# One graph-attention kernel, second attention of a group: two tasks of two banks joined into one task of four banks

## Chip, cores, metric

The kernel runs on one core of one Trainium2 chip. The metric is device time in microseconds (us). TensorE is PE below, ScalarE ACT, VectorE DVE, GpSimd POOL. In this kernel matmuls read tiles in the memory called SBUF and write their results into "banks", tiles in the memory called PSUM; reading a finished bank out with ACT or DVE is called its evacuation. Times are medians of unprofiled and profiled executions of one call; a profile is one execution. All runs told of here were in the fast state, with a granted TensorE clock of 0.998 or 0.999 of full speed.

## The reference

Inputs are 128 graphs of 64 nodes with 512 features, one shared adjacency matrix, and the weights of one layer. Cut to what matters:

```python
def gat_heads(x, adj, W, a):                     # W: [H, F, O]
    Wh = einsum('bnf,hfo->bhno', x, W)
    f1 = einsum('bhno,ho->bhn', Wh, a[:, :O]); f2 = ... a[:, O:]
    e = f1[..., :, None] + f2[..., None, :]
    e = where(e > 0, e, 0.01 * e)                # leaky ReLU
    e = where(adj[None, None] > 0, e, -1e9)
    return einsum('bhnm,bhmo->bhno', softmax(e), Wh)

h   = relu(layernorm(x))
h1  = elu(gat_heads(h, adj, W_heads, a_heads))   # four heads, then concatenated
out = elu(gat_heads(h1, adj, W_out, a_out))      # the second attention
y   = relu(out @ w1 + b1) @ w2 + b2 + out
return x + layernorm(y)
```

## The kernel before

The 128 graphs are worked through in 16 groups of 8. Each large product is done as seven smaller block products, p = 1, 5, 6, 2, 3, 7, 4 in that order. One product p of one head is a "step" on PE: four f32 matmuls of 256 columns, which leave eight records in the trace. Blocks c11, c12, c21, c22 of the result come out of sums of the banks g1, g5, g6 (DVE) and of copies s1, s5, t (ACT). Shortened:

```python
def after(p):                                    # evacuation of product p
    if p in (1, 5, 6):
        if p == 6:
            nc.vector.tensor_tensor(gb[6], gb[6], sb["s1"], ALU.add)
        nc.scalar.copy(sb[nm], gb[p])            # s1, s5 or t
    elif p == 2: post("c11", gb[1])
    elif p == 7: post("c22", gb[6], sb["s5"], gb[1])     # c22 = g6 + s5
    elif p == 3: post("c12", gb[5], sb["t"], gb[5])
    else:        post("c21", gb[6])              # p = 4 adds into bank g6

def elu(dst, src, name):                         # three scratch tiles
    ex = wk.tile([P, 512], FP, tag="elu", name=f"ex{name}", bufs=3)
    nc.scalar.activation(ex, src, AF.Relu, scale=-1.0)
    nc.scalar.activation(ex, ex, AF.Exp, scale=-1.0)
    nc.vector.scalar_tensor_tensor(dst, ex, -1.0, src, ALU.add, ALU.max)
```

So p = 4 of a head may not start before the DVE addition c22 has read g6. Each head's last product, p = 4, is put off ("late") into the next head's second step; that of the last head falls into the next product, `project2`, whose pieces of g_b are on PE by then:

```python
return [
    s[0], lambda: (s[1](), flush_late()), lambda: (s[2](), next_sums()), s[3], s[4],
    lambda: (s[5](), late.append(s[6])),
]                                                # next_sums: three GpSimd subtractions
...
    flush_late()                                 # after the last head
```

The second attention of the group before runs beside these steps, from a list of entries spread evenly over the 24 steps of the four heads (`gap` is an empty entry):

```python
def attend2(g, q):                               # half a group: two banks
    pa = [aux([P, FO], ...) for b in range(NB)]
    ... 4 matmuls of 64 x 64 tiles, 512 columns each ...
    for b in range(NB):
        elu(OUT[g][:, 2 * q + b], pa[b], f"2_{g}_{q}_{b}")

gap + score + [lambda: spread2(g)] + gap * 2 + [lambda: softmax2(g)] + gap * 5
+ [lambda: transpose_weights2(g)] + gap * 2 + attend[0:1] + gap * 2 + attend[1:2] + gap * 4
```

The second softmax has two operations that will matter. L435 is the leaky ReLU, which reads the tile `e` twice; L453 multiplies a mask by the reciprocal sums. Both have both inputs in SBUF:

```python
nc.vector.scalar_tensor_tensor(ei, ei, ALPHA, ei, ALU.mult, ALU.max)          # L435
...
nc.vector.tensor_tensor(rb, blkones[...], r[...], ALU.mult)                   # L453
```

Of the kernel before, what the change touches and what calls it, by code (L numbers as in the profile page):

```python
# [9 lines left out]
FP = mybir.dt.float32  # L10
# [12 lines left out]
def gat_preln_kernel(  # L23
# [31 lines left out]
    P = 128  # L55
# [3 lines left out]
    FO = W_out.shape[1]  # L59
    DF = w1.shape[1]  # L60
    NB = P // N
    KC = F // P
    NT = B * N // P
    G = 4
# [9 lines left out]
    big = ctx.enter_context(tc.tile_pool(name="big", bufs=1))  # L74
# [5 lines left out]
    def bank(name):  # L80
        return ps.tile([P, 2, T], FP, tag="mm", name=name)

    def flat(ap):
        return ap.rearrange("p a b -> p (a b)")
# [8 lines left out]
    def aux(shape, name):  # L93
        return ps.tile(shape, FP, tag="aux", name=name, bufs=2)
# [473 lines left out]
    def elu(dst, src, name):  # L568
# [5 lines that stand above are left out]
# [130 lines left out]
    A2, AT2, F2, OUT = {}, {}, {}, {}  # L704

    def scores2(g, j):
        if j == 0:
            F2[g] = sm.tile([P, 2, G], FP, tag="f2", name=f"f2_{g}")
        f = F2[g]
        for c in range(2):  # L710
            junk = wk.tile([P, FO], FP, tag="elu", name=f"jf{g}_{j}_{c}", bufs=3)
            nc.vector.scalar_tensor_tensor(
                junk, WH2[g][:, j], 1.0, ao[:, c, :], ALU.mult, ALU.mult,
                accum_out=f[:, c, j:j + 1],
            )

    def spread2(g):

        f = F2[g]
        dg = sm.tile([P, G, N], FP, tag="s2dg", name=f"s2dg{g}", bufs=1)  # L720
        nc.vector.tensor_tensor(
            dg, eye[:, None, :].to_broadcast([P, G, N]), f[:, 1][:, :, None].to_broadcast([P, G, N]),
            ALU.mult,
        )
        F2[g] = f, dg

    def softmax2(g):
        f, dg = F2.pop(g)
        pe = aux([P, G, N], f"s2pe{g}")
        nc.tensor.matmul(  # L730
            pe.rearrange("p h m -> p (h m)"), blkones.rearrange("p b n -> p (b n)"),
            dg.rearrange("p h m -> p (h m)"), start=True, stop=True,
        )
        A2[g] = softmax(pe, f[:, 0], G, "s2", g)

    def transpose_weights2(g):
        A = A2.pop(g)
        pt = aux([P, G, P], f"s2pt{g}")
        for j in range(G):
            nc.tensor.transpose(pt[:, j, :], A[:, j].rearrange("p b m -> p (b m)"), ident)  # L740
        AT2[g] = wk.tile([P, G, P], FP, tag="hT", name=f"at2_{g}", bufs=4)
        nc.scalar.copy(AT2[g], pt)

    def attend2(g, q):


        if q == 0:
            tag = "out" if g < NG - 1 else "z11"
            OUT[g] = big.tile([P, G, FO], FP, tag=tag, name=f"o{g}")
        pa = [aux([P, FO], f"pa2_{g}_{q}_{b}") for b in range(NB)]  # L750
        for b in range(NB):
            rows = slice(b * N, (b + 1) * N)
            for c in range(2):
                nc.tensor.matmul(
                    pa[b][c * N:(c + 1) * N], AT2[g][rows, 2 * q + c, rows],
                    WH2[g][rows, 2 * q + c, :], start=True, stop=True, skip_group_check=True,
                )
        for b in range(NB):
            elu(OUT[g][:, 2 * q + b], pa[b], f"2_{g}_{q}_{b}")

    def stage_e(g):

        gap = [lambda: None]
        score = [lambda j=j: scores2(g, j) for j in range(G)]
        attend = [lambda q=q: attend2(g, q) for q in range(2)]
        return (
            gap + score + [lambda: spread2(g)] + gap * 2 + [lambda: softmax2(g)] + gap * 5
            + [lambda: transpose_weights2(g)] + gap * 2 + attend[0:1] + gap * 2 + attend[1:2] + gap * 4
        )


# [169 lines left out]
    for g in range(NG):  # L941
        if g >= 1:
            side = stage_e(g - 1)
            done, n = 0, 6 * H
            for i in range(n):
                if i % 6 == 0:
                    steps = project1(g, i // 6)
                steps[i % 6]()
                while done * n < (i + 1) * len(side):
                    side[done]()  # L950
                    done += 1
            flush_late()
# [3 lines left out]
        if g == NG - 1:  # L956
            run(project2(g), tr + [nothing] * 6 + ff[:2])
            run(ff[2:], [
                lambda: [scores2(g, j) for j in range(G)], lambda: spread2(g), nothing, nothing,
                lambda: softmax2(g), *[nothing] * 7, lambda: transpose_weights2(g), nothing,  # L960
                *[lambda q=q: attend2(g, q) for q in range(2)], nothing,
            ])
            continue
# [67 lines left out]
```

## Time and profile before

| | before |
|---|---|
| time, median of 3 runs | 2299.97 us (2298.76 to 2300.67) |
| span of the profiled execution | 2297.4 us |
| busy share PE, DVE, ACT, POOL | 99%, 56%, 39%, 44% |
| distance from one group to the next ("period") | 140.37 us |
| second softmax: L435 on s2e, L453 on s2rb (medians of 16) | 0.42 us, 0.17 us |

PE is busy throughout, so the kernel's time is the sum of the distances between the starts on PE. The period is the sharpest ruler: the distance between the single softmax product (L730) of one group and that of the next. It repeats to 0.03 us over twelve groups. Whole executions are less steady: the first such product starts 178.3 to 181.9 us after the beginning in the eleven profiles (1.7 us of that spread is only that the softmax stands one step later in four of them; a mark ahead of it, the first of the products `pzS`, starts at 126.1 to 128.0 us), and the thirteenth distance is 0.2 to 1.2 us longer than the others (why, was not looked into). I give both, period and time; differences of periods are taken before rounding.

The line of the page for the products that p = 4 belongs to has no idle time in it. Columns: line, engine, operation, tiles, shapes, count, then busy us, mean ns, then idle us before them and its cause.

```profile
L289 PE MATMUL g_a<-z,w 128*128 128x256 f32 x1440 | 341.8, 380 | 0.0
```

The list leaves out waits below about 0.15 us. The 0.1 us that the prediction found before p = 4 is therefore not in it.

### The profile page before, as it was taken

Reading aid. Unit: us, or ns where it says so; the run is one execution under the profiler, and the core shown is the slowest. Engines: PE = TensorE matmul, PEld = TensorE weight load, DVE = VectorE, ACT = ScalarE, POOL = GpSimd, SP = SyncE. Lnnn points to the kernel's source line nnn. Section 1 sums busy time; section 2 is a strip of 40 time slices with the busy share of each in tenths; the row PEclk is TensorE's granted clock in tenths of the full one; section 3 lists DMA queues with packets and bytes.
Section 4 is the critical chain, followed back from the end, with each engine's and each line's share of the span. In section 5 each row is a group of like instructions: output and inputs, shape, how many; then the busy total and the mean of one; then the engine's idle time right before and its main releaser. Section 6 shows DMA issues by size and latency. Waiting matters only on the chain. (4 is left out here: it accounts for less than half of the span.)

```text
span 2297.4 us, 33255 instructions
## 1 busy us (share of the span) xinstructions
PE 2274.2 (99%) x11856; PEld 1892.9 (82%) x11856; DVE 1278.8 (56%) x2226; ACT 904.4 (39%) x1633; POOL 1019.9 (44%) x906
## 2 busy tenths in 40 slices
PE   8999999999999999999999999999999999999997
PEld 4688888888888888888888888888888888888885
DVE  7555554755546555564655546555475554744427
ACT  3435344252442525335253352534425244251512
POOL 7653534435244442644425344353443525533324
PEclk9999999999999999999999999999999999999999
DMA  7554454644546455464544645445454454635543
GB/s 280 197 180 130 146 180 133 183 133 142 176 133 183 137 150 167 133 184 133 161 152 141 181 133 178 132 145 180 132 182 133 143 178 131 183 119 170 161 146 106
DMA packets 255011, 361.14 MB, mean 157 GB/s; under 512 B 23768, under 2 KB 143608, under 8 KB 254848
## 3 DMA queue, kind: packets, MB, share of 16 engines
q1 hardware_dynamic: 249744, 341.16, 48.5%
q0 software_dynamic: 4576, 16.81, 2.0%
q8 instruction: 96, 1.57, 0.3%
q10 hardware_dynamic: 528, 1.05, 0.1%
q14 instruction: 67, 0.55, 0.1%
HBM read 331.66 MB, written 27.26 MB: 156 GB/s over the span
## 5 line engine op out<-in xcount | busy, mean ns | idle before, releaser
L304 PE MATMUL g_b<-w,h 128*128 128x256 f32 x2560 | 593.2, 380 | 0.0
L304 PEld LDWEIGHTS g_b<-w,h 128*128 128x128 f32 x2560 | 481.7, 190 | 64.0 <-issue 2.0
L289 PE MATMUL g_a<-z,w 128*128 128x256 f32 x1440 | 341.8, 380 | 0.0
L289 PE MATMUL g_a<-zs_z,w 128*128 128x256 f32 x1440 | 336.0, 382 | 0.0
L289 PEld LDWEIGHTS g_a<-zs_z,w 128*128 128x128 f32 x1440 | 270.3, 190 | 58.9 <-issue 24.3
L289 PEld LDWEIGHTS g_a<-z,w 128*128 128x128 f32 x1440 | 272.6, 190 | 41.0 <-DVE g_a L603 4.9
L304 PE MATMUL g_b<-w,hS 128*128 128x256 f32 x1024 | 238.2, 380 | 0.0
L607 POOL TENSOR_TENSOR hS<-hS,h 128x512 f32<-128x512 f32 x60 | 78.2, 1303 | 359.7 <-DVE hS L573 359.7
L304 PEld LDWEIGHTS g_b<-w,hS 128*128 128x128 f32 x1024 | 192.3, 190 | 24.7 <-issue 0.2
L571 ACT ACTIVATE exc<-g_a 128x512 f32<-128x512 f32 x240 | 142.5, 594 | 164.3 <-DVE g_a L603 96.3
L573 DVE SCALAR_TENSOR_TENSOR h<-exc,g_a 128x512 f32<-128x512 f32 x180 | 123.6, 687 | 140.8 <-ACT exc L572 140.2
L572 ACT ACTIVATE exc<-exc 128x512 f32<-128x512 f32 x240 | 151.4, 631 | 6.6
L688 POOL TENSOR_TENSOR h<-h,h 128x512 f32<-128x512 f32 x64 | 86.8, 1365 | 138.6 <-PE g_b L304 138.6
L688 POOL TENSOR_TENSOR h<-hS,h 128x512 f32<-128x512 f32 x64 | 81.7, 1277 | 146.7 <-PE g_b L304 146.4
L314 POOL TENSOR_TENSOR zs_z<-zS,z 128x512 f32<-128x512 f32 x60 | 85.1, 1418 | 134.1 <-PE g_a L289 130.8
L489 ACT COPY at<-s1pt 128x512 f32<-128x512 f32 x64 | 34.4, 589 | 272.0 <-PE s1pt L485 272.0
L830 POOL TENSOR_TENSOR xr<-xr,bs 128x512 f32<-128x512 f32 x64 | 98.2, 1538 | 81.5 <-DMA xr<-in_x_dram 44.1
L304 PE MATMUL g_d<-w,rt 128*128 128x256 f32 x512 | 121.8, 380 | 2.1 <-DVE o L822 1.0
L289 PE MATMUL g_c<-ot,w 128*128 128x256 f32 x512 | 122.8, 383 | 0.6 <-DVE ot L792 0.6
L289 PE MATMUL g_a<-zS,w 128*128 128x256 f32 x480 | 113.4, 379 | 0.0
L304 PEld LDWEIGHTS g_d<-w,rt 128*128 128x128 f32 x512 | 97.0, 190 | 17.1 <-DVE o L822 2.3
L315 POOL TENSOR_TENSOR zs_z<-z,zs_z 128x512 f32<-128x512 f32 x60 | 81.2, 1353 | 65.1 <-PE g_a L289 44.4
(164 smaller groups left out, 3553.5 us busy)
## 6 DMA issues: line engine op xcount, KB each, us to landing
w<-tc SPq DMA_DIRECT2D x624, 256.0 KB, 2.7
w<-in_L_gnn_W_out_dram SPq DMA_DIRECT2D x192, 256.0 KB, 2.7
w<-in_L_gnn_W_heads_dram SPq DMA_DIRECT2D x180, 256.0 KB, 3.1
w<-in_L_gnn_w_dram SPq DMA_DIRECT2D x96, 256.0 KB, 2.7
x<-in_x_dram SPq DMA_DIRECT2D x64, 256.0 KB, 4.6
xr<-in_x_dram SPq DMA_DIRECT2D x128, 128.0 KB, 2.7
out_dram<-o SPq DMA_DIRECT2D x128, 128.0 KB, 2.4
tc<-pt POOLq DMA_DIRECT2D x20, 512.0 KB, 4.3
```

The costliest lines, as they stand in the source:

```text
L289: LAST["pe"] = nc.tensor.matmul(bk[:, o, :], w[:, k, ts(o, P)], a[:, k, :], start=start and o == 0 and k == 0, stop=k == 1, skip_group_che ...
L304: LAST["pe"] = nc.tensor.matmul(bk[:, j, :], a[:, k, ts(j, P)], w[:, k, :], start=start and k == 0 and j == 0, stop=i == len(ms) - 1 and k ...
L314: eng.tensor_tensor(s2, s1, a11, ALU.subtract)
L315: eng.tensor_tensor(s4, a12, s2, ALU.subtract)
L489: nc.scalar.copy(AT[t].rearrange("p b h n -> p (b h) n"), pt)
L571: nc.scalar.activation(ex, src, AF.Relu, scale=-1.0)
L572: nc.scalar.activation(ex, ex, AF.Exp, scale=-1.0)
L573: nc.vector.scalar_tensor_tensor(dst, ex, -1.0, src, ALU.add, ALU.max)
L607: nc.gpsimd.tensor_tensor(dst, dst, H1["22"][:, h], ALU.add)
L688: nc.gpsimd.tensor_tensor(dst[:, h], x0[:, h], x1[:, h], ALU.subtract)
L830: nc.gpsimd.tensor_tensor(xr, xr, bs, ALU.add)
```

## The change

The intent is to enter and leave PE's mode of four 64 x 64 tiles once per group, not twice. All eight matmuls of a group stand in one block, into four banks: two from the pool for small results and two from the ring of the large products. The task is placed in the third step of the last head. The list has 24 entries where it had 25.

```diff
--- before.py
+++ after.py
@@ -747,7 +747,17 @@
         if q == 0:
             tag = "out" if g < NG - 1 else "z11"
             OUT[g] = big.tile([P, G, FO], FP, tag=tag, name=f"o{g}")
-        pa = [aux([P, FO], f"pa2_{g}_{q}_{b}") for b in range(NB)]
+        second_attention(g, q, [aux([P, FO], f"pa2_{g}_{q}_{b}") for b in range(NB)])()
+
+    def attend2_all(g):
+
+        OUT[g] = big.tile([P, G, FO], FP, tag="out", name=f"o{g}")
+        pa = [[aux([P, FO], f"pa2_{g}_0_{b}") for b in range(NB)]]
+        pa.append([flat(bank(f"pa2_{g}_1_{b}")) for b in range(NB)])
+        for finish in [second_attention(g, q, pa[q]) for q in range(2)]:
+            finish()
+
+    def second_attention(g, q, pa):
         for b in range(NB):
             rows = slice(b * N, (b + 1) * N)
             for c in range(2):
@@ -755,17 +765,19 @@
                     pa[b][c * N:(c + 1) * N], AT2[g][rows, 2 * q + c, rows],
                     WH2[g][rows, 2 * q + c, :], start=True, stop=True, skip_group_check=True,
                 )
-        for b in range(NB):
-            elu(OUT[g][:, 2 * q + b], pa[b], f"2_{g}_{q}_{b}")
+
+        def finish():
+            for b in range(NB):
+                elu(OUT[g][:, 2 * q + b], pa[b], f"2_{g}_{q}_{b}")
+        return finish
 
     def stage_e(g):
 
         gap = [lambda: None]
         score = [lambda j=j: scores2(g, j) for j in range(G)]
-        attend = [lambda q=q: attend2(g, q) for q in range(2)]
         return (
             gap + score + [lambda: spread2(g)] + gap * 2 + [lambda: softmax2(g)] + gap * 5
-            + [lambda: transpose_weights2(g)] + gap * 2 + attend[0:1] + gap * 2 + attend[1:2] + gap * 4
+            + [lambda: transpose_weights2(g)] + gap * 5 + [lambda: attend2_all(g)] + gap * 3
         )
```

## The prediction

> **What bounds the kernel now.** I read the page first, for the busy shares.
>
> ```profile
> PE 2274.2 (99%) x11856; PEld 1892.9 (82%) x11856; DVE 1278.8 (56%) x2226; ACT 904.4 (39%) x1633; POOL 1019.9 (44%) x906
> ```
>
> The columns are busy us, share of the 2297.4 us span, instructions. TensorE (PE) is the bound. The list of waits puts next to no waiting on PE between 150 and 2020 us (0.5 us in all), the distance from one group's second attention to the next group's is constant (478.71 to 619.08 to 759.44 us, 140.4 each), and the granted clock there is 1.00. So the kernel's time is the sum of the distances between PE's starts, and a change counts by what it does to that sum. Busy shares cannot show it, since ends of matmuls are modelled; I therefore read starts in the timeline of PE around one group's last two tasks. Columns: start, length, engine, line, tiles, shapes, records (an f32 matmul leaves two records).
>
> ```profile
> 485.01 1.89 PE L289 MATMUL g_a<-z,w 128*128 128x256 f32 x8
> 486.83 1.09 PE L754 MATMUL pa<-wh,at 64*64 64x512 f32 x8
> 487.85 1.99 PE L289 MATMUL g_a<-zs_z,w 128*128 128x256 f32 x8
> 489.68 1.89 PE L289 MATMUL g_a<-z,w 128*128 128x256 f32 x8
> 491.41 3.62 PE L289 MATMUL g_a<-zs_z,w 128*128 128x256 f32 x16
> 494.86 1.03 PE L304 MATMUL g_b<-w,h 128*128 128x256 f32 x4
> 495.82 1.99 PE L289 MATMUL g_a<-z,w 128*128 128x256 f32 x8
> ```
>
> A full step of 8 records takes 1.727 us (491.41 to 494.86 is two). The step before the attention takes 1.82, the attention 1.02, the step after it 1.83: the task costs 4.67 - 2 x 1.727 = 1.22 us. Its four 64x64 matmuls run side by side as two passes of 512 columns; two passes at full rate (4 x 0.216, from the 256-column records) would be 0.86. So 0.36 us of a task is getting into and out of the four-tile mode. The second fact is small: the four g_b records at 494.86 should take 0.86, but the next step starts 0.96 later. That is a stall of 0.10 us per group, too short to be listed as a wait.
>
> The first score product is a control for "is that 0.36 paid per block or per pass": eight matmuls of 256 columns, thus four passes, in the same mode.
>
> ```profile
> 540.89 1.89 PE L304 MATMUL g_b<-w,h 128*128 128x256 f32 x8
> 542.71 1.09 PE L405 MATMUL s1pe<-R,L 64*64 64x256 f32 x16
> 543.74 1.99 PE L289 MATMUL g_c<-ot,w 128*128 128x256 f32 x8
> 545.57 2.75 PE L304 MATMUL g_b<-w,h 128*128 128x256 f32 x12
> ```
>
> It costs 545.57 - 540.89 - 2 x 1.727 = 1.23 us against 4 x 0.216 = 0.86: again 0.36, though it has twice the passes. The overhead is paid once per block.
>
> What holds the step at 495.82 is seen on ScalarE (ACT) and VectorE (DVE), three stretches of their timelines in the same group:
>
> ```profile
> 480.20 0.59 ACT L571 ACTIVATE ex<-pa 128x512 f32<-128x512 f32 x1
> 480.68 0.63 ACT L572 ACTIVATE exc<-exc 128x512 f32<-128x512 f32 x1
> 481.20 0.63 ACT L572 ACTIVATE ex<-ex 128x512 f32<-128x512 f32 x1
> ...
> 491.86 0.58 ACT L255 COPY t_a<-g_a 128x512 f32<-128x512 f32 x1 [1.36 <-DVE g_a L254]
> 492.34 0.60 ACT L571 ACTIVATE exc<-g_a 128x512 f32<-128x512 f32 x1
> 492.97 0.63 ACT L572 ACTIVATE exc<-exc 128x512 f32<-128x512 f32 x1
> ```
>
> ```profile
> 491.13 0.69 DVE L254 TENSOR_TENSOR g_a<-g_a,s_a 128x512 f32<-128x512 f32 x1
> 493.63 0.69 DVE L573 SCALAR_TENSOR_TENSOR h<-exc,g_a 128x512 f32<-128x512 f32 x1 [1.81 <-ACT exc L572]
> 494.24 0.69 DVE L603 TENSOR_TENSOR g_a<-g_a,t_a 128x512 f32<-128x512 f32 x1
> 495.06 0.70 DVE L603 TENSOR_TENSOR g_a<-g_a,s_a 128x512 f32<-128x512 f32 x1
> ```
>
> The last product of the last head (p = 4) accumulates into bank g6, which the DVE addition at 495.06 (c22 = g6 + s5) must read first. PE goes on at 495.82, 0.76 after that addition began. The addition itself began 0.20 after the p = 7 step ended (494.86). In the other heads p = 4 comes two steps later and never waits; in the last head only half a g_b piece, 0.86 us, stands between.
>
> **What the Trainium skill says.** "TensorEngine Tiling (Array Packing)", Key Properties: changing the tiling mode drains TensorE, changing only the tile doesn't. The trace agrees: 0.36 us per block, for two passes and for four. "TensorE: Matmul & The Clock Gate", Architectural detail, says ACT and DVE are strict FIFO while PE can pull only weight loads ahead. That decides the case: whatever the scheduler puts in front on ACT or DVE delays what stands behind it, and PE cannot step around a blocked matmul. The 0.10 us stall agrees.
>
> **The change part by part.** It applies to groups 0 to 14; group 15 keeps its two tasks. Matmuls, evacuations and transfers keep their number and shapes.
>
> Removed: one of two blocks. One block then has four passes of 512 columns: 1.22 + 0.86 = 2.08 us where two blocks took 2.44. That is 0.36 per group, 15 x 0.36 = 5.4 us.
>
> Moved: the schedule of the second stage has 24 entries instead of 25, so scores and softmax come about one step later, and both attentions come after the third product (p = 6) of the last head. By the built kernels' bank addresses and instruction order, the two banks from the ring were last used by the previous head or earlier and are read out about two steps before; ring rotation later in the group stays served by banks freed in time. Those waits are free.
>
> Added: the evacuation of four banks as one burst, eight ACT and four DVE operations, placed by the scheduler in front of the last head's first ELU (c11). The order on ACT is now copy t, relu, relu, exp, exp, relu, relu, exp, exp, then c11's relu and exp; on DVE: g6 += s1, four outputs o, h11, g5 += t, c22. The scratch tile of the ELU has three buffers, so the fourth relu also waits for the first o. I count from A, the end of the p = 6 step, with intervals from the lines above: step end to reader 0.20; relu to own exp 0.63; relu or copy to an unrelated operation 0.48; exp to next 0.52; exp to the DVE operation that reads it 0.66; DVE to DVE 0.60; DVE to ACT 0.73.
>
> The previous head's c21 ends on PE at A - 1.73; its relu, exp and DVE part follow at -1.53, -0.90, -0.24. Then g6 += s1 at 0.37 and copy t at 1.10. The burst: relu 1.58, relu 2.07, exp 2.55, exp 3.07, relu 3.59, relu 4.08 (its buffer is free at about 3.93, from the first o at 3.21 plus 0.73), exp 4.57, exp 5.09. Then c11 relu 5.61, exp 6.24, on DVE h11 6.90, g5 += t 7.50, c22 8.10, and with 0.76 PE may start p = 4 at 8.86. PE itself would be ready after the block (2.08), three steps (5.18) and half a piece (0.86), at 8.12. So it stalls about 0.74 us, visible as an idle gap, where before it was 0.10.
>
> The sum per group: before, two blocks 2.44 + three steps 5.18 + 0.86 + 0.10 = 8.58; after, 8.86. That is +0.28 us, times 15 = +4.2 us. The saved 0.36 is not gained at all: it only makes PE reach the blocked step sooner. After p = 4 everything stands relative to PE as before, so I expect nothing to be recovered: PE has no other slack in the group.
>
> **The rivals.** First, the burst is hidden and the full 5.4 us come out, 2294.6 us. For it: ACT is busy only 39% of the span and DVE 56%. Against: that is an average, and the edge above already stalls by 0.10 with c11 at the head of the queue. Second, a middle way: if the chain is shorter than I count by 0.03 per ACT interval, its ten or so links give back 0.3, the net is about zero, about 2300 us. The intervals are measured, so I give this little. Third, a further wait on top: the burst delays the copies of the following attention products out of their banks. Against: the last ELU relu of the head waits for p = 4 itself (0.20 after it), so behind it ACT has caught up; this would need 1 us more per group (about 2319 us) and I see nothing for it. Fourth, transfers: unchanged in number and no PE wait on them is listed; nothing.
>
> **Range and chances.** 2299.97 + 4.2 = 2304.2, taken as 2304. An error of 0.15 us per group in the chain is 2.3 us, and runs spread by 2 us; 2300 to 2307 should hold it, with the low side kept for the middle way. Two per cent is 46 us, which is 3 us per group; no way that I see leads there.
>
> **What would show it.** In the changed trace: one block of 16 attention records per group, lasting about 1.88 us from its start to the next step's start (right: block overhead paid once); a listed PE wait before a g_a matmul on DVE's c22 addition, about 0.5 to 0.7 us, 15 times; eight ACT operations in a row between copy t and c11; the group period longer by about 0.3 us, 140.65 instead of 140.37. I am wrong if the period is 140.0 and no wait appears, if the block takes much over 1.9 us, or if a wait stands on a bank of the ring.

## The result, and the profile after

| | before | after |
|---|---|---|
| time, same call, 6 runs each | 2300.04 us (2298.76 to 2300.67) | 2305.88 us (2305.12 to 2307.09) |
| span of the profiled execution | 2297.4 us | 2305.2 us |
| period | 140.37 us | 140.82 us |
| L435 on s2e, L453 on s2rb (medians of 16) | 0.42, 0.17 us | 1.38, 1.21 us |

The ratio is 1.0027, 95% interval [1.0014, 1.0040]: slower by 0.27%, far inside 2%. A ratio here is the mean time of one kernel's fast runs over that of the other's of the same rounds, so it is not quite the ratio of the medians in the tables.

First the page of the kernel after, the row of groups that answers to the one above: the products into g_a now have listed idle time, and its cause is c22 (L603).

```profile
L289 PE MATMUL g_a<-z,w 128*128 128x256 f32 x1440 | 345.0, 382 | 8.7 <-DVE g_a L603 8.7
```

The timeline of PE in the kernel after, around the task. Columns: start, length, engine, line, tiles, shapes, records, and in brackets the idle time with its cause.

```profile
488.83 1.95 PE L764 MATMUL pa<-wh,at 64*64 64x512 f32 x16
490.70 1.99 PE L289 MATMUL g_a<-z,w 128*128 128x256 f32 x8
492.54 3.62 PE L289 MATMUL g_a<-zs_z,w 128*128 128x256 f32 x16
495.99 1.03 PE L304 MATMUL g_b<-w,h 128*128 128x256 f32 x4
497.58 1.99 PE L289 MATMUL g_a<-z,w 128*128 128x256 f32 x8 [0.56 <-DVE g_a L603]
```

One block of 16 records takes 490.70 - 488.83 = 1.87 us from start to start. The four g_b records should take 0.86 and the next step follows 497.58 - 495.99 = 1.59 after them: PE lost 0.73 us there. The bracket says 0.56, since the ends of matmuls are modelled; distances of starts are safer.

The timeline of ACT in the same kernel shows what holds c22. A, the end of the p = 6 step, is 488.74 (the end of that step's eight records at full rate, 0.09 before the block starts).

```profile
489.83 0.59 ACT L255 COPY t_a<-g_a 128x512 f32<-128x512 f32 x1 [1.36 <-DVE g_a L254]
490.31 1.09 ACT L571 ACTIVATE ex<-pa 128x512 f32<-128x512 f32 x2
...
493.27 1.18 ACT L572 ACTIVATE ex<-ex 128x512 f32<-128x512 f32 x2
494.31 0.62 ACT L571 ACTIVATE exc<-g_a 128x512 f32<-128x512 f32 x1
```

And DVE, which gets the exp of c11 only after that:

```profile
495.63 0.69 DVE L573 SCALAR_TENSOR_TENSOR h<-exc,g_a 128x512 f32<-128x512 f32 x1 [0.38 <-ACT exc L572]
496.24 0.69 DVE L603 TENSOR_TENSOR g_a<-g_a,t_a 128x512 f32<-128x512 f32 x1
496.84 0.69 DVE L603 TENSOR_TENSOR g_a<-g_a,s_a 128x512 f32<-128x512 f32 x1
```

ACT is never idle between copy t and c11's relu: eight operations of the attention stand in one burst (each line with x2 is two of them). c11's relu starts at A + 5.57, c22 at A + 8.10, and PE goes on at A + 8.84.

That accounts for 0.28 us of the period. The period grew by 0.46. A comparison of all distances of starts finds the rest elsewhere, in another head, near p = 4 as well. First PE in the kernel before, at that head's p = 4 and the step in front of it:

```profile
609.91 1.89 PE L289 MATMUL g_a<-zS,w 128*128 128x256 f32 x8
611.64 1.89 PE L289 MATMUL g_a<-z,w 128*128 128x256 f32 x8
```

The same two in the kernel after:

```profile
611.67 1.89 PE L289 MATMUL g_a<-zS,w 128*128 128x256 f32 x8
613.47 1.99 PE L289 MATMUL g_a<-z,w 128*128 128x256 f32 x8
```

The step should take 1.73 and p = 4 starts 1.80 later: a stall of 0.07. The record after the restarting one comes 320 ns later, where 216 is normal, so the stall costs 0.07 + 0.10, 0.18 before rounding. Before the change this p = 4 did not wait: 611.64 - 609.91 is 1.73. The queue of DVE ahead of it explains why. Kernel before, DVE:

```profile
602.94 0.42 DVE L435 SCALAR_TENSOR_TENSOR s2e<-s2e 128x256 f32<-128x256 f32 x1
...
605.93 0.17 DVE L453 TENSOR_TENSOR s2rb<-blkones,s2r 128x8 f32<-128x8 f32 x1
...
608.38 0.70 DVE L603 TENSOR_TENSOR g_a<-g_a,s_a 128x512 f32<-128x512 f32 x1 [0.35 <-PE g_a L289]
```

Kernel after, DVE, the same operations:

```profile
606.21 1.38 DVE L435 SCALAR_TENSOR_TENSOR s2e<-s2e 128x256 f32<-128x256 f32 x1
...
610.27 1.21 DVE L453 TENSOR_TENSOR s2rb<-blkones,s2r 128x8 f32<-128x8 f32 x1
...
612.72 0.69 DVE L603 TENSOR_TENSOR g_a<-g_a,s_a 128x512 f32<-128x512 f32 x1
```

Kernel after, POOL:

```profile
605.81 1.49 POOL L607 TENSOR_TENSOR hS<-hS,h 128x512 f32<-128x512 f32 x1
...
610.19 1.27 POOL L316 TENSOR_TENSOR zs_z<-z,zs_z 128x512 f32<-128x512 f32 x1 [0.38 <-PE g_a L289]
```

Before, c22 (L603, the last line) waited for PE itself and began 3.26 us ahead of the p = 4 that needs it (which started at 611.64). After, it began 0.75 us ahead. L435 and L453 grew from 0.42 and 0.17 to 1.38 and 1.21 us, 2.00 us together. Each begins inside a POOL operation and ends when that one ends: 607.59 against 607.30, and 611.48 against 611.46 (POOL times are rough). The reduction between them, L436, stayed at 0.42, but had no POOL operation beside it. Another reduction, L439, did begin inside one (L315, 608.53 to 609.81), at 609.62, and took 0.41; before the change it took 0.42. The Trainium skill, "SBUF — State Buffer", section "Who interferes with whom", says that a DVE instruction with two SBUF inputs contends with a GpSimd instruction that reads SBUF, and that a `tensor_reduce` doesn't contend; the summary of the same page says that the second one to issue fully blocks until the first finishes. The durations agree to 0.15 us: the POOL operation's end plus 0.42 would be 607.72 for L435 (607.59 measured), plus 0.17 would be 611.63 for L453 (611.48). Whether it is the operands that do it is tested below.

The order matters too, and for L435 it is what changed. In the kernel before, L435 also ran beside L607 in 15 of the 16 groups, but began 0.16 us ahead of it (602.94 against 603.11 here) and took 0.42. In the kernel after it begins 0.40 us behind the start of L607. L453 had no POOL operation beside it before the change.

### The profile page after: what moved, and what is told of

Same layout as the page of the kernel before. It is cut to its first block, busy times and chain, and to the rows that moved or that the text cites. A ratio compares the mean times of both kernels' runs of the same rounds, so it can differ in the third digit from the quotient of the medians.

```text
span 2305.2 us, 33275 instructions
## 1 busy us (share of the span) xinstructions
PE 2273.2 (99%) x11856; PEld 1892.3 (82%) x11856; DVE 1316.6 (57%) x2226; ACT 905.3 (39%) x1633; POOL 1019.4 (44%) x906
## 5 line engine op out<-in xcount | busy, mean ns | idle before, releaser
L289 PE MATMUL g_a<-zs_z,w 128*128 128x256 f32 x1440 | 330.4, 379 | 0.0
L607 POOL TENSOR_TENSOR hS<-hS,h 128x512 f32<-128x512 f32 x60 | 79.4, 1324 | 260.4 <-DVE hS L573 260.4
L712 DVE SCALAR_TENSOR_TENSOR jf<-wh,ao 128x512 f32<-128x512 f32 x128 | 118.6, 961 | 7.8 <-ACT wh L694 7.6
L315 POOL TENSOR_TENSOR zs_z<-z,zs_z 128x512 f32<-128x512 f32 x60 | 81.6, 1360 | 70.2 <-PE g_a L289 47.8
```

Source lines behind the costliest of these rows:

```text
L289: LAST["pe"] = nc.tensor.matmul(bk[:, o, :], w[:, k, ts(o, P)], a[:, k, :], start=start and o == 0 and k == 0, stop=k == 1, skip_group_che ...
L315: eng.tensor_tensor(s4, a12, s2, ALU.subtract)
L607: nc.gpsimd.tensor_tensor(dst, dst, H1["22"][:, h], ALU.add)
L712: nc.vector.scalar_tensor_tensor(junk, WH2[g][:, j], 1.0, ao[:, c, :], ALU.mult, ALU.mult, accum_out=f[:, c, j:j + 1],)
```

## The experiments

Theory: the change saves 0.36 us per group with the block, loses 0.64 at the last head's p = 4 through the burst, and loses 0.18 in the other head through the later softmax. Rivals: all of it is the burst; or the shift acts through scores, ring or place and not through GpSimd; or the restart of 0.10 us belongs to the boundary and isn't lost by a stall. Nine runs were timed in five rounds or more, the change itself among them, beside the kernel before in the same call. All were correct, and all ratios lie within 2% of 1. In the first call the kernel before took 2299.44 us (9 runs), in the second 2299.41 (9), in the third 2299.21 (18).

| run | time, us | to before of its call | period, us | period's change x 15 |
|---|---|---|---|---|
| aligned | 2303.06 | +3.6 | 140.65 | +4.2 |
| shift_only | 2303.27 | +3.8 | 140.54 | +2.6 |
| split_one_later | 2290.30 | -9.1 | 139.81 | -8.3 |
| early | 2294.63 | -4.8 | 140.01 | -5.4 |
| after_again | 2305.59 | +6.2 | 140.82 | +6.9 |
| softmax_back | 2302.38 | +3.0 | 140.64 | +4.1 |
| p4_later | 2296.50 | -2.9 | 140.17 | -2.9 |
| aligned_p4_later | 2290.96 | -8.5 | 139.81 | -8.3 |
| psum_operands | 2303.54 | +4.3 | 140.64 | +4.1 |

**aligned.** The change with one empty entry more, so that scores, softmax and attention stand where they stood before.

```diff
-  + [lambda: transpose_weights2(g)] + gap * 5 + [lambda: attend2_all(g)] + gap * 3
+  + [lambda: transpose_weights2(g)] + gap * 6 + [lambda: attend2_all(g)] + gap * 3
```

> The changed kernel with one more empty entry in the schedule of the second stage (25 as in the kernel before), so that scores and softmax stand where they stood and only the attention is one block of four banks in the third step of the last head. Theory (two stalls: the burst in front of the last head's c22 addition, and two VectorE softmax operations that now run under GpSimd operations and hold up head 1's p = 4): the second stall goes, the first stays at about 0.73 us; the group period falls from 140.82 to 140.65 us, the two softmax operations are back at 0.42 and 0.17 us, total about 2303.5 to 2304.5. Rival (the schedule's shift is free and all of the loss comes with the burst): period stays 140.82 and the time about 2305.9.

Measured 2303.06 (2302.50 to 2303.72), ratio 1.0016 [1.0004, 1.0029]. The period is 140.65: +0.28, exactly the prediction's sum. L435 and L453 are back at 0.42 and 0.17, and the stall in the other head is gone. The stall at the last head's p = 4 is unchanged (945 ns from the last g_b record to p = 4, 943 to 948 in the change).

**shift_only.** The kernel before with its list shortened to 24 entries and nothing joined.

```diff
-  ... + gap * 2 + attend[0:1] + gap * 2 + attend[1:2] + gap * 4
+  ... + gap * 2 + attend[0:1] + gap * 2 + attend[1:2] + gap * 3
```

> The kernel before with one entry less at the end of the schedule (24 as in the changed kernel): still two tasks of two banks, but scores, softmax and both tasks about one step later. Theory: the softmax operations at their lines 435 and 453 grow to about 1.4 and 1.2 us, head 1's p = 4 stalls by 0.17 us (0.07 of wait and 0.10 of restart), period 140.37 + 0.17 = 140.54 us, total about 2302.5 to 2303. The burst of two banks is too short to hold up the last head. Rival (shift is free): period 140.37, about 2300.

Measured 2303.27 (2302.51 to 2303.68), ratio 1.0017 [1.0003, 1.0030]: slower by 0.3 us more than I had allowed. The period is +0.18, L435 and L453 take 1.37 and 1.21 us. So the shift costs by itself, with two separate tasks as before.

**early.** Aligned, with the joined task two steps earlier.

```diff
-  ... + gap * 6 + [lambda: attend2_all(g)] + gap * 3
+  ... + gap * 4 + [lambda: attend2_all(g)] + gap * 5
```

> As aligned, but the block stands two steps earlier, after the first step of the last head, with all four banks evacuated in one burst. Theory: the burst now stands in front of work that PE reads no sooner than two or more steps later, so no stall: period 140.01 us, about 2294.6. Rival (a burst of eight ScalarE operations costs the same wherever it stands): period 140.65, about 2304. Rival of banks (six banks are too few while the last head and the attention hold five): a listed wait of PE on a VectorE evacuation in the step after the block.

Measured 2294.63 (2293.46 to 2295.77), ratio 0.9979 [0.9967, 0.9992]. Period -0.36: the saved mode change comes out whole once the burst no longer stands in front of c11. Here p = 4 of the last head waits as it did in the kernel before, 308 ns against 216.

**split_one_later.** Aligned, one block, but the ELUs of the second two banks entered one step later.

```diff
-        for finish in [second_attention(g, q, pa[q]) for q in range(2)]:
-            finish()
+        first, FIN2[g] = [second_attention(g, q, pa[q]) for q in range(2)]
+        first()
...
-  ... + gap * 5 + [lambda: attend2_all(g)] + gap * 3
+  ... + gap * 6 + [lambda: attend2_all(g), lambda: FIN2.pop(g)()] + gap * 2
```

> As aligned, but of the four banks only the first two are evacuated at once; the other two are entered one step later, behind the last head's first ELU. One block of matmuls as before. Theory: the c22 addition is held up no more than in the kernel before (0.10 us), so the whole 0.36 us of the saved block comes out: period 140.01 us, 15 x 0.36 = 5.4 us, about 2294.6. Rival (the block of four banks itself, or the two banks from the ring, costs what was saved): period 140.3 or more, about 2300 or more.

Measured 2290.30 (2289.64 to 2291.06), ratio 0.9961 [0.9948, 0.9973]. This was right in direction and 4 us too good. The trace shows why:

```profile
493.13 1.46 PE L304 MATMUL g_b<-w,h 128*128 128x256 f32 x6
494.43 1.89 PE L289 MATMUL g_a<-z,w 128*128 128x256 f32 x8
```

The scheduler put p = 4 behind six g_b records in place of four, which are 1.30 us where c22 needs 0.96. So the small stall that the kernel before had is gone too: 0.09 of wait, and the 320 ns record after it. That is 0.195 us per group or 2.9 us, if the slow record is really part of the stall (5.4 and 2.9 make the 8.3 of the period; the 0.8 more in the time is of the size of the runs' spread). This was a guess from one trace, so p4_later tests it alone.

**p4_later.** The kernel before, unjoined, with the last head's p = 4 behind a whole piece of g_b.

```diff
-        return unit(f"b{g}", product_n(...), post, (1, 5, 6, 2, 7, 3, 4))
+        parts = unit(f"b{g}", product_n(...), post, (1, 5, 6, 2, 7, 3, 4))
+        part0 = parts[0]
+        parts[0] = lambda: (part0(), flush_late())
+        return parts
...
-            flush_late()                          # after the last head
```

> The kernel before with p = 4 of the last head behind a whole g_b piece (eight records, 1.73 us) in place of half of one. The addition c22 is then done 0.77 us before PE needs it. If a stall costs its wait and a slow restart (0.09 + 0.104 us per group), 15 of them give 2.9 us: 2296.5. If only the wait is lost and the 320 ns record belongs to every such boundary, 1.4 us: 2298.0. If the later c21 makes a new wait, no gain or a loss.

Measured 2296.50 (2295.86 to 2297.49), ratio 0.9989 [0.9976, 1.0001]; the interval touches 1, the period doesn't waver: 140.17, -0.20. The record after p = 4's first now comes after 216 ns. So a stall of 0.09 us cost 0.195, and the rival (1.4 us in all) falls.

**aligned_p4_later.** Aligned, with the full burst in front of c11, and p = 4 put off as in p4_later.

> One block of four banks, full burst of eight ScalarE and four VectorE operations in front of c11 as in the change, schedule aligned as before, and p = 4 behind a whole g_b piece. PE then reaches p = 4 at 2.08 + 5.18 + 1.73 = 8.99 us after A, c22 lets it go at 8.86. If the whole loss of the change in the third step is this one wait, all comes out: -5.4 -1.4 -1.6 = 2291.1 us. Rival: the burst delays something else as well, and 2294 or more remain.

Measured 2290.96 (2290.86 to 2291.14), ratio 0.9964 [0.9952, 0.9977]. Its timeline of PE:

```profile
486.01 1.95 PE L767 MATMUL pa<-wh,at 64*64 64x512 f32 x16
...
493.17 1.89 PE L304 MATMUL g_b<-w,h 128*128 128x256 f32 x8
494.90 1.89 PE L289 MATMUL g_a<-z,w 128*128 128x256 f32 x8
```

The eight g_b records take 494.90 - 493.17 = 1.73, full rate: no stall. c22 began at 494.01, 0.89 ahead. The same burst, which cost 0.64 us per group in the change, costs nothing here. So the loss in the third step was this one wait, and nothing else that the burst delays. This run and split_one_later are the fastest of all; it is ahead by 8.5 us against before and, over the two medians of one call, by 14.6 against the change.

**after_again.** The change once more, in the call of the last runs.

> The changed kernel once more, in the same call as the runs below. If the two costs are independent (the aligned schedule alone cost +3.6 us, the shift alone +3.8 us against the kernel before), it should be +7.4 us, about 2306.9. If it repeats the first measurement, it is +5.8 us, about 2305.3, and the two costs partly cover one another.

Measured 2305.59 (2305.16 to 2306.07), ratio 1.0028 [1.0015, 1.0041]: +6.2, between the two. By the periods the costs add: +0.28 and +0.18 give +0.46, as measured. That the two times add up to a microsecond more is within what the first 180 us and the odd interval near the end vary by. I don't read more into it.

**softmax_back.** The change with only the softmax one entry earlier.

```diff
-  ... [lambda: spread2(g)] + gap * 2 + [lambda: softmax2(g)] + gap * 5
+  ... [lambda: spread2(g)] + gap + [lambda: softmax2(g)] + gap * 6
```

> The changed kernel with the second softmax alone one schedule entry earlier, where it stood before the change; scores, spread and attention stay one later. If the cost of the shift is those two VectorE operations meeting GpSimd's, then L435 on s2e is back at 0.42 us and L453 on s2rb at 0.17, the stall before p = 4 of head 1 is gone, and the time falls by 2.2 to 3.8 us from the changed kernel's, to about 2303. Rival: the shifted scores or the ring cost it, and the time stays at that of the changed kernel.

Measured 2302.38 (2301.95 to 2304.04), ratio 1.0014 [1.0000, 1.0027], 3.2 us below after_again of the same call. L435 and L453 are at 0.42 and 0.17, the stall of the other head is gone, the period is 140.64. It isn't the shifted scores: their products with the vector `ao` (L712) were lengthened by the shift from 774 ns on average to 961, and in this run they still take 985, at no cost. But in this run L435 is again 0.16 us ahead of L607, L453 has no POOL operation beside it, and the whole softmax is further from c22: it doesn't separate the meeting with GpSimd from the place.

**psum_operands.** The change, with the order on PE, ACT and POOL untouched. One input of L435 and one of L453 come from PSUM.

```diff
-                nc.vector.tensor_tensor(ei, pe, f1[...], ALU.add)
-                nc.vector.tensor_tensor(ei, ei, mask, ALU.add)
-            nc.vector.scalar_tensor_tensor(ei, ei, ALPHA, ei, ALU.mult, ALU.max)
+                nc.vector.tensor_tensor(pe, pe, f1[...], ALU.add)      # in PSUM
+                nc.vector.tensor_tensor(ei, pe, mask, ALU.add)
+                nc.vector.tensor_tensor(pe, pe, mask, ALU.add)         # one more
+                r = ri = pe[:, 0, 0:q]
+            nc.vector.scalar_tensor_tensor(ei, ei, ALPHA, ei if f1 is None else pe, ...)
```

> The changed kernel with the order of PE, ScalarE and GpSimd untouched. Only in the second softmax, one input each of the leaky-ReLU operation and of the rb operation lies in PSUM in place of SBUF (one more VectorE addition of about 0.43 us is needed for it). If the two operations were held by GpSimd because both their inputs lie in SBUF, they take about 0.42 and 0.2 us at the same places, c22 of head 1 begins about 1.6 us earlier (2.0 less 0.43), the stall before p = 4 of head 1 is gone, the group period is 140.65 and the time is 2.2 to 3.8 us below the changed kernel's, about 6.0 less, so +3.0 on the kernel before: 2302 to 2303.5. If the later place of the softmax is what costs, its two durations or at least the period of 140.82 stay, and the time is about 2305.6.

Measured 2303.54 (2302.17 to 2304.47, 14 runs), ratio 1.0019 [1.0011, 1.0027]. By the differences to before of each call, that is 1.9 us below after_again, a little less than the 2.2 expected at least; the period fell from 140.82 to 140.64, 2.7 us over 15 groups. Its DVE timeline (the source lines stand two lower, and L455 is the old L453):

```profile
605.25 0.42 DVE L437 SCALAR_TENSOR_TENSOR s2e<-s2e,s2pe 128x256 f32<-128x256 f32 x1
...
608.54 0.16 DVE L455 TENSOR_TENSOR s2rb<-blkones,s2pe 128x8 f32<-128x8 f32 x1
...
609.95 0.69 DVE L605 TENSOR_TENSOR g_a<-g_a,s_a 128x512 f32<-128x512 f32 x1
```

At the later place and in the same order, with an operation more, the first takes 0.42 again, though POOL had L609 from 604.49 to 605.77. The second takes 0.16, but it ended 0.18 before its POOL neighbour (L316 at 608.88) started, so its own operand is not tested here. The next operation shows the lock the other way round: L462 has two SBUF inputs, ran from 608.74 to 609.43, and L316, begun inside it, took 1.68 us in place of 1.27 (POOL times are rough). c22 begins at 609.95, 2.14 ahead of its p = 4 (612.09), and PE doesn't stall there. So the later place alone does no harm; the two SBUF inputs of L435 under a GpSimd operation start the delay.

Two builds did not come to a run. Four scratch buffers for the ELU did not fit into the pool (13.1 KB asked, 11.3 left), so whether three bind was not tried; the trace of the change speaks against it, as the fourth relu followed the third at once. The first form of psum_operands, with both inputs of L435 in PSUM, was refused when building.

## Why the prediction was right or wrong

**The time** was predicted at 2304.0, range 2300 to 2307, and measured at 2305.88 and 2305.59. "Within 2%" was right. Two steps of the prediction decide the difference to the kernel before, one right and one wrong. That the time still lies in the range is partly luck: the range was made for errors of the chain, and a loss of 2.6 us that the prediction held to be nothing happened to fit into it.

**Removed: the mode change is paid once per block, 0.36 us per group.** Right. The block took 1.87 us against 1.88 predicted, and early, which has the saving and no new stall, shows -0.36 in the period.

**Added: the burst holds c11, c22 and p = 4.** Right, to a few hundredths, in this chain from A:

| event | predicted | measured |
|---|---|---|
| copy t | 1.10 | 1.09 |
| relu of c11 | 5.61 | 5.57 |
| h11 on DVE | 6.90 | 6.89 |
| c22 | 8.10 | 8.10 |
| p = 4 on PE | 8.86 | 8.84 |

aligned, which has this step and not the shift, shows +0.28 in the period as predicted, and aligned_p4_later shows that it is this wait: when only PE's order changes, it is gone. What the Trainium skill says in "TensorE: Matmul & The Clock Gate", section "Architectural detail", and what the prediction drew from it, held: behind the burst ACT did not bring c11 forward. c11's product was done on PE by 492.54, where the next step starts, and its relu began at 494.31, after the burst. The fourth relu did not wait for a scratch buffer, as the prediction's times had it (buffer free at 3.93, relu at 4.08).

**Moved: "Those waits are free", and in the other heads p = 4 "never waits".** This step failed. I looked at the ring's banks for the shift and not at what the shifted DVE work meets. The shift made two operations of the softmax begin inside two GpSimd operations; they became 2.00 us longer together, the slack of 3.26 us between c22 and p = 4 of another head was used up, and p = 4 there lost 0.18 us per group, 2.6 us in all. shift_only shows the cost without the joined task, softmax_back and psum_operands remove it from the change in two different ways. The later place used part of the slack and the blocking the rest. In psum_operands 2.14 us of slack are left, so the place alone would have been harmless.

**The small stall of 0.10 us** was read right as a wait, but the prediction counted only half of it. The slow record after it, 0.104 us, is lost too. It was in both sums alike and so did not hurt the difference; in split_one_later it made me miss 2.9 of the gain.

**The rivals.** The full gain of 5.4 us did not come, for the reason given against it. The middle way fell. "A further wait on top" was named, but in the wrong place: I looked for it at the attention's copies. Transfers play no part: neither the waits on PE nor the periods show one.

## What to carry to other kernels

When PE is full, a saving on PE is worth only what the next wait leaves of it: before joining tasks, follow the evacuations on ACT and DVE that the joined task puts in front of the next operation PE needs, and give PE other work to do first where that chain is longer; here moving one product by half a piece turned +3.6 us into -8.5. When a schedule shifts by one step, compare for the moved DVE operations with two SBUF inputs what GpSimd does at their new time and which of the two begins first: 0.16 us ahead cost L435 nothing, 0.40 us behind cost it 0.96 us. Measure in the distance between repeating starts; it repeated to 0.03 us per group where whole times of one kernel spread by about 2 us.

## What the Trainium skill lacked or had wrong

- "TensorEngine Tiling (Array Packing)", Key Properties, says that a change of tiling mode drains TensorE and gives no size. Here a block of four-tile work cost 0.36 us beyond its passes, once per block, for two, four passes of 512 columns and four of 256 alike; joining two blocks gave 0.36 us per group back (early).
- No page I found has the restart after a stall. A 128 x 128 f32 product of 256 columns that PE had to wait for sends its second record 320 ns after the first in place of 216, also after a wait of only 0.07 or 0.09 us. Taking away a wait of 0.09 us per group gained 0.195 (p4_later). The same 320 ns record follows a block of four-tile work, so it is a part of the 0.36 above.
- "SBUF — State Buffer", Who interferes with whom, was right and decisive: 0.42 to 1.38 us and 0.17 to 1.21 us for two SBUF inputs, 0.41 for a reduction that began under a GpSimd operation (L439), 0.42 with one input from PSUM under a GpSimd operation, and 0.42 with two SBUF inputs where DVE began first. What it doesn't say is how small an operation is hit: eight values per partition waited 1.04 us.
- No page I found warns that a list of waits drops the short ones. Waits of 0.07 to 0.10 us on PE were in no list here, and were worth 2.6 and 2.9 us in the whole kernel.
